# A graph attention and a DiT block on one core: graph maxima moved to PSUM, both outputs in one pair of banks, and four steps placed elsewhere in the written order

## The chip, the cores and the metric

The kernel runs on one core of one Trainium2 chip. The metric is the device time of one execution in microseconds (us); lower is better. Before the change three runs took 708.34, 708.88 and 709.95 us, median 708.88.

## What is computed

The inputs are x with 64 graphs of 64 nodes and 256 features, a condition of 256 features for each graph, an integer adjacency of 64 x 64 x 11 for each graph, and weights. All arithmetic is fp32. Two blocks follow each other; the reference, cut to what matters:

```python
# 1. graph attention, M = 20 neighbours, H = 16 heads, two directions d
q_exp = where(v.sum(-1) == 0, 0, q)            # condition of each node
self_feat = concat([v, q_exp]) @ W_self.T + b_self
kv = self_feat[:, :20]
for d in range(2):                             # adjacency, or transposed
    aff = qh @ kh / 4                          # heads of 16 features
    aff = where(A.sum(-1) > 0, aff, NEG) + A @ w_bias + b_bias
    output += (softmax(aff) @ kv) @ Wout[d] + bout[d]
x = v + relu(self_feat + output)
# 2. DiT block; shift, scale, gate come from silu(cond) @ Wt + bt
h = layernorm(x) * (1 + scale_msa) + shift_msa
x = x + gate_msa * (attention(h) @ Wproj + bproj)     # 16 heads, 64 tokens
h = layernorm(x) * (1 + scale_mlp) + shift_mlp
x = x + gate_mlp * (gelu(h @ W1 + b1) @ W2 + b2)
```

## The kernel before

**Groups, tiles and slots.** The 64 graphs are taken in nine groups (`NB`, line 26): 4, seven times 8, and 4 graphs. A group of 8 has 512 tokens in four tiles of 128. The order of all work is written out by hand: the scheduler is switched off (line 72), so each engine executes its instructions in the order in which the Python functions issue them, and waits in place for what an instruction needs. `start` (line 987) brings in groups 0 and 1, then for g = 1 to 7 a `boundary(g)` (line 826) and a `period(g)` (line 927) follow, then `finish` (line 1106).

In `period(g)` three stages of three groups run together: the DiT attention of group g, the graph attention of group g + 1 and the MLP of group g - 1; group g + 2 is prepared as well. The period has a slot for each of the four tiles, and `slot` (line 781) fixes what one does:

- TensorE writes the scores of a DiT tile (L657) and of a graph tile (L493) to two pairs of PSUM banks, `sca` (tag "pa") and `scb` (tag "pb"). DiT scores take columns 0 to 255 of each bank, graph scores 256 to 415.
- `block_exp`: VectorE takes maxima (L668) and subtracts them (L670), ScalarE the exponential (L674). `block_normal`: sum (L678), reciprocal (L679), GpSimd's product (L680).
- `graph_masked`: VectorE multiplies scores by the mask into `w` (L504), GpSimd adds the term (L509). `graph_exp`: maxima into `mx` in SBUF (L514), subtraction in `w` (L515), exponential (L516). `graph_normal`: L521, L522, L523.
- The tiles of the slot before are finished: transposes (ppT, L687, and pwT, L531), `block_attended` into a new pair "pao" with tag "pa" (L698, evacuated by ScalarE at L708), and `graph_output` into a new pair "po" with tag "pb" (L549; evacuated by L556, or L558 and L559; GpSimd adds at L560).

Between these lie places named p, f0, f1, d0, f2, f2b, d1, d2 and f3, and `fills` (line 948) says which further steps stand in each place of each slot: `mlp_up` (pu, L749, with its gelu L751), `mlp_down` (py, L759), `block_proj` (pproj, L731, then L721 and L740), `mlp_gated` and `mlp_out` (L721, L773 and the output DMA L775), LayerNorms, mask steps (L382 to L395), and the making of group g + 2's features: `self_cond` (on GpSimd, two products tq, L350, that need row flags fetched by a DMA, nzb), `self_product` (pf, L359) and `self_features` (L366 on VectorE, which empties pf's bank, and a copy to kv on GpSimd, L367).

A LayerNorm is three steps: `norm_stats` (L578, L579, then four small GpSimd operations to L585), `normed` (xn on ScalarE, L591) and `modulated` (phT on TensorE, L599; L602 on VectorE; L606 on GpSimd). `half_normed` and `second_normed` call them for the first and the second LayerNorm; hT and h2T hold the results, and `block_qk` (pqk, L619) reads hT.

**Banks.** Four PSUM banks beside the two pairs are handed out in turn by `bank` (line 90); py keeps one for as long as it accumulates. A step that gets a bank waits until the one that had it last has been read. In the second slot of a steady period the two pf get the same bank, as only two others are handed out between them.

**Buffers by tag.** A new tile of a tag waits until every reader of the one before it is done. So the scores of a slot wait for the evacuation of "pao" and "po" of the slot before.

**DMA.** Loads, gates and outputs are issued on SP, in the written order. `load_gate` brings the gates that `biased` (L714, on GpSimd) and `gated` (L721) read.

Of the kernel before, what the change touches and what calls it, by code (L numbers as in the profile page):

```python
# [9 lines left out]
F32 = mybir.dt.float32  # L10
# [7 lines left out]
P = 128  # L18
# [28 lines left out]
def graph_attention_then_dit_block(  # L47
# [49 lines left out]
    def pair(which, name):  # L97
        return ps.tile([P, 2, 512], F32, tag=which, name=name)
# [383 lines left out]
    def graph_scores(g, j, sc, first=4 * N):  # L482

        G = groups[g]
        t = Tile()
        t.g, t.j = g, j
        t.pa = [p_[:, :, ds(first, 8 * M)] for p_ in sc]
        kblk = G.kblk[j]
        for d in range(2):
            for c in range(2):  # L490
                for r in range(2):
                    for s in range(2):
                        nc.tensor.matmul(  # L493
                            t.pa[d][ts(s, N), r, ts(c, 4 * M)],
                            G.qT[ts(r, 64), d, c, ds(j * P + s * N, N)],
                            kblk[ts(r, 64), d, c, s, :], start=True, stop=True,
                        )
        return t
# [11 lines left out]

    def graph_exp(t):
        wf = t.w.rearrange("p h d m -> p (h d) m")
        mx = small.tile([P, 2 * H], F32, tag="mx", name="mx")
        nc.vector.tensor_reduce(mx, wf, AX.X, ALU.max)  # L514
        nc.vector.tensor_tensor(wf, wf, mx.unsqueeze(2).to_broadcast([P, 2 * H, M]), ALU.subtract)  # L515
        nc.scalar.activation(wf, wf, AF.Exp)  # L516
# [264 lines left out]
    def slot(e, c, e_next, c_next, before, fill):  # L781
        Eb, Cb = before
        fill("p")
        sc = [pair("pa", "sca"), pair("pb", "scb")] if e or c else None
        E = block_scores(*e, sc) if e else None
        C = graph_scores(*c, sc) if c else None
        if Eb:
            block_turned(Eb)
        elif Cb:
            graph_turned(Cb[0])  # L790
        fill("f0")
        if e_next:
            block_keys(*e_next)
        if c_next and c_next[0] != 1:
            graph_keys(*c_next)
        if E:
            block_exp(E)
        if c_next and c_next[0] == 1:
            graph_keys(*c_next)
        if C:  # L800
            graph_masked(C)
        fill("f1")
        if Eb and Cb:
            graph_turned(Cb[0])
        if E:
            block_normal(E)
        fill("d0")
        if C:
            graph_exp(C)
        if Eb:  # L810
            block_attended(Eb, pair("pa", "pao")[:, 0])
        fill("f2")
        po = pair("pb", "po") if Cb else None
        for i, t in enumerate(Cb):
            if i > 0:
                graph_turned(t)
            graph_output(t, po[:, i])
        fill("f2b")
        fill("d1")
        if C:  # L820
            graph_normal(C)
        fill("d2")
        fill("f3")
        return E, [C] if C else []

    def boundary(g, before):

        Eb, Cb = before
        n, a = g + 1, g + 2
        G, A = groups[g], groups[g - 1]  # L830
        last = A.nt // 2 - 1
        graph_k(n, 0)
        if g >= 2:
            mlp_gated(g - 2, len(groups[g - 2].parts) - 1)
        graph_v(n, 1)
        if g == 2:
            second_normed(g - 1, 0, 0)
        for i in range(0 if g == 2 else 4, 7):
            mask_step(n, i)
        if g >= 2:  # L840
            mlp_out(g - 2, len(groups[g - 2].parts) - 1)
        block_turned(Eb)
        for t in Cb:
            graph_turned(t)
        if g == 2:
            second_normed(g - 1, 0, 1)
        graph_q(n, 0, 0)
        block_attended(Eb, pair("pa", "pao")[:, 0])
        for t in Cb:
            graph_output(t, pair("pb", "po")[:, 0])  # L850
        graph_v_spread(n)
        graph_q(n, 0, 1)
        if last:
            second_normed(g - 1, 0, 2)
        if a < NG:
            load_adj(a)
            load_x(a)
        to_tokens(g, 1)
        if a < NG:
            load_xT(a)  # L860
        norm_stats(G, G.x1[1])
        block_proj(g - 1, last, later=True)
        normed(G, G.x1[1])
        block_added(g - 1, last)
        graph_q(n, 1, 0)
        graph_k(n, 1)
        modulated(G, G.hT, 1, amp1, off1, g)
        graph_q(n, 1, 1)
        second_normed(g - 1, last, 0)
        graph_keys(n, 0)  # L870
        block_qk(g, 1, 0)
        block_qk(g, 1, 1)
        block_keys(g, 0)
        second_normed(g - 1, last, 1)
        block_qk(g, 0, 0)
        second_normed(g - 1, last, 2)
        block_qk(g, 0, 1)
        block_v(g, 0)
        if a < NG:
            nonzero_rows(a)  # L880
        if g >= 2 and a < NG:
            mask_step(a, 0)
        load_gate(0, g, 0)
        for j2 in range(A.nt // 2):
            load_gate(1, g - 1, j2)
# [16 lines left out]
    def second_normed(g, j2, step):  # L902

        G = groups[g]
        if step == 0:
            second[g] = Tile()
            norm_stats(second[g], G.x1[j2])
        elif step == 1:
            normed(second[g], G.x1[j2])
        else:  # L910
            if j2 == 0:
                G.h2T = new_hT("hT" if g == NG - 1 else "h2T")
            modulated(second[g], G.h2T, j2, amp2, off2, g)
# [13 lines left out]
    def period(g):  # L927

        m, n, a = g - 1, g + 1, g + 2
        G = groups[g]  # L930

        def up(*ms):
            return [(mlp_up, m, i) for i in ms]

        def down(part, *ms):
            return [(mlp_down, m, part) + ms] if part < len(groups[m].parts) else []

        def masks(*steps):
            return [(mask_step, a, i) for i in steps] if g > 1 and a < NG else []

        def ahead(f, *args):
            return [(f, a) + args] if a < NG else []

        def bias_2(j2):
            return [(biased, 1, m, j2)] if j2 < len(groups[m].parts) else []

        gated_0 = [(mlp_gated, m, 0), (mlp_out, m, 0)] if g > 1 else []
        fills = [
            {
                "f1": [(block_v, g, 1)],  # L950
                "d2": masks(1) + ahead(self_cond, 0) + ahead(self_cond, 1),
                "f3": up(0, 1) + (up(2, 3) if g > 1 else []),
            },
            {
                "f0": ahead(self_product, 0) + (up(2, 3) if g == 1 else []) + down(0, 0, 1),
                "f1": ahead(self_features, 0),
                "f2b": ahead(self_product, 1),
                "d1": ahead(self_features, 1),
                "d2": masks(2, 3) + [(biased, 0, g, 0)],
                "f3": up(4, 5),  # L960
            },
            {
                "f0": down(0, 2, 3),
                "f1": down(0, 4, 5),
                "f2": ahead(graph_v, 0),
                "d2": bias_2(0) if g > 1 else [],
                "f3": [(block_proj, g, 0)] + up(6, 7),
            },
            {
                "f0": [(half_normed, n, 0)] + down(0, 6) + [(load_gate, 0, g, 1)],  # L970
                "f1": down(0, 7) + gated_0 + [(half_normed, n, 1)],
                "d0": [(half_normed, n, 2)],
                "f2": down(1, 0, 1, 2),
                "f2b": [(second_normed, g, 0, 0)] if g > 1 else [],
                "d2": bias_2(1 if g > 1 else 0),
                "f3": down(1, 3, 4) + [(half_normed, n, 3)] + ([(second_normed, g, 0, 1)] if g > 1 else []) + down(1, 5, 6, 7)
                + [(biased, 0, g, 1)],
            },
        ]
        if n == NG - 1:  # L980

            fills = fills[:3]
            fills[2]["f3"] = [(block_proj, g, 0)] + up(6) + [(half_normed, n, 0)] + up(7) + [(half_normed, n, 1), (load_gate, 0, g, 1)]
        slots = [((g, j), (n, j) if j < groups[n].nt else None) for j in range(G.nt)]
        return run_slots(slots, fills, (None, []))

    def start():
# [71 lines left out]
        for t in t1:  # L1059
# [36 lines left out]
                "f2": [(graph_v, 2, 0)],  # L1096
                "d0": [(half_normed, 1, 2)],
                "f2b": [(load_gate, 0, 0, 0)],
                "f3": [
                    (time_projection, 4), (biased, 0, 0, 0), (half_normed, 1, 3), (time_projection, 5),  # L1100
                ],
            },
        ]
        return run_slots([((0, 0), (1, 2)), ((0, 1), (1, 3))], fills, (None, t1))
# [154 lines left out]
```

## Time and profile before

| | |
|---|---|
| median of 3 runs | 708.88 us (708.34 to 709.95) |
| the profiled execution's own time | 711.31 us |
| its span, first to last instruction | 709.5 us |
| mean granted TensorE clock | 0.983 |
| TensorE busy with matmuls | 671.2 us, 95% |
| VectorE, ScalarE, GpSimd busy | 453.1, 377.0, 435.5 us |
| first scores of periods 1 to 7 at | 114.7, 194.9, 275.3, 355.1, 435.7, 515.8, 592.4 us |

Lines of the profile are read thus. A line of a stage has the stretch in us from the span's start, its length, then busy time and number of instructions for PE (matmuls), PEld (weight loads), DVE (VectorE), ACT (ScalarE) and POOL (GpSimd), then the granted TensorE clock (1.00 is full), the DMA engines' share and GB/s. A line of the order in time has start and duration in us, the engine, the source line, the operation, output <- input, their shapes and a count of instructions drawn together; brackets at the end give the idle time of the engine just before and what ended it. fp32 matmuls appear as two passes each. The end of a matmul is modelled: two that follow each other overlap in the listing, and their pace is the distance of their starts.

### The profile page before, as it was taken

Reading aid. Unit: us, or ns where it says so; the run is one execution under the profiler, and the core shown is the slowest. Engines: PE = TensorE matmul, PEld = TensorE weight load, DVE = VectorE, ACT = ScalarE, POOL = GpSimd, SP = SyncE. Lnnn points to the kernel's source line nnn. Section 1 sums busy time; section 2 is a strip of 40 time slices with the busy share of each in tenths; the row PEclk is TensorE's granted clock in tenths of the full one; section 3 lists DMA queues with packets and bytes.
Section 4 is the critical chain, followed back from the end, with each engine's and each line's share of the span. In section 5 each row is a group of like instructions: output and inputs, shape, how many; then the busy total and the mean of one; then the engine's idle time right before and its main releaser. Section 6 shows DMA issues by size and latency. Waiting matters only on the chain.

```text
span 709.5 us, 16045 instructions
## 1 busy us (share of the span) xinstructions
PE 671.2 (95%) x6624; PEld 456.8 (64%) x6624; DVE 453.1 (64%) x755; ACT 377.0 (53%) x675; POOL 435.5 (61%) x501
## 2 busy tenths in 40 slices
PE   8998899897999999999999999999999989899997
PEld 7655565585566765577556775568566765567576
DVE  4968845679388755878488755878378755654210
ACT  3353444665465654765465654666466645854412
POOL 7446345667657675668658675678557684547430
PEclk9997999999999999999999999999999999999999
DMA  9345140310441140410431240510321240011210
GB/s 283 103 123 175 53 141 2 76 46 13 136 83 25 60 147 3 105 46 21 144 69 37 61 128 21 106 46 20 90 69 30 56 113 2 3 46 29 77 43 30
DMA packets 45712, 50.74 MB, mean 72 GB/s; under 512 B 6761, under 2 KB 32937, under 8 KB 45641
## 3 DMA queue, kind: packets, MB, share of 16 engines
q1 hardware_dynamic: 44040, 48.26, 24.8%
q8 instruction: 52, 0.85, 0.6%
q0 software_dynamic: 368, 0.60, 0.4%
q10 hardware_dynamic: 1232, 0.87, 0.4%
q14 instruction: 20, 0.16, 0.1%
HBM read 42.63 MB, written 7.09 MB: 70 GB/s over the span
## 4 chain that ended last, share of the span: by engine, by line
PE 57%; DVE 15%; ACT 9%; POOL 8%; DMA 7%; issue 3%; SPq 0%; ACTq 0%; POOLq 0%; DVEq 0%
PE py L759 12%; PE pqk L619 7%; PE pu L749 7%; PE pqT L457 5%; DVE w L515 4%; PE pproj L731 4%; PE ppT L687 3%; PE pwT L531 3%; DMA nzd<-nz 3%; DMA nzb<-nzd 2%; PE pf L359 2%; PE phT L599 2%; PE po L549 2%; PE pk L442 2%; DVE mx L514 2%
## 5 line engine op out<-in xcount | busy, mean ns | idle before, releaser
L759 PE MATMUL py<-w,u 128*128 128x256 f32 x512 | 123.0, 386 | 0.2 <-ACT u L751 0.2
L749 PE MATMUL pu<-h2T,w 128*128 128x512 f32 (+1 forms) x256 | 108.2, 567 | 0.2 <-POOL h2T L606 0.2
L759 PEld LDWEIGHTS py<-w,u 128*128 128x128 f32 x512 | 95.4, 192 | 17.3 <-issue 3.8
L509 POOL TENSOR_TENSOR w<-w,term 128x640 f32<-128x640 f32 x32 | 49.4, 1546 | 63.4 <-DVE w L504 23.8
L749 PEld LDWEIGHTS pu<-h2T,w 128*128 128x128 f32 x256 | 48.4, 191 | 46.5 <-issue 44.4
L680 POOL TENSOR_TENSOR pr<-pr,sm 128x1024 f32<-128x1024 f32 x32 | 60.8, 1900 | 10.5 <-DVE sm L679 8.8
L751 ACT ACTIVATE u<-pu,vec 128x512 f32<-128x512 f32 (+1 forms) x72 | 43.2, 639 | 44.4 <-PE pu L749 44.3
L516 ACT ACTIVATE w<-w 128x640 f32<-128x640 f32 x32 | 23.4, 734 | 76.8 <-DVE w L515 76.8
L591 ACT ACTIVATE xn<-x,shift,rstd 128x256 f32<-128x256 f32 x64 | 34.8, 592 | 51.5 <-POOL shift L585 51.5
L619 PE MATMUL pqk<-hT,wqkv 128*128 128x512 f32 (+1 forms) x144 | 58.7, 551 | 3.2 <-POOL hT L606 3.2
L457 PE MATMUL pqT<-sfT,wq 128*128 128x512 f32 (+1 forms) x144 | 60.8, 550 | 0.0
L560 POOL TENSOR_TENSOR xT<-xT,sfT 128x256 f32<-128x256 f32 x32 | 23.7, 742 | 59.7 <-ACT sfT L559 37.4
L523 POOL TENSOR_TENSOR w<-w,sm 128x640 f32<-128x640 f32 x32 | 43.4, 1358 | 27.0 <-DVE sm L522 27.0
L515 DVE TENSOR_TENSOR w<-w,mx 128x640 f32<-128x640 f32 x32 | 52.9, 1653 | 1.1
L678 DVE TENSOR_REDUCE sm<-pr 128x16 f32<-128x1024 f32 x32 | 38.8, 1212 | 22.1 <-ACT pr L674 20.2
L602 DVE TENSOR_TENSOR h2T<-phT,amp 128x512 f32<-128x512 f32 x15 | 10.4, 690 | 58.1 <-PE phT L599 58.1
L687 PE MATMUL ppT<-ident,pr 128*128 128x128 f32 x256 | 37.2, 285 | 10.3 <-ACT u L751 4.5
L674 ACT ACTIVATE pr<-pr 128x1024 f32<-128x1024 f32 x32 | 33.8, 1058 | 22.6 <-DVE pr L670 22.4
L714 POOL TENSOR_TENSOR x<-x,gates 128x512 f32<-128x512 f32 x32 | 42.4, 1325 | 5.1 <-DMA gates<-gate 5.1
L619 PEld LDWEIGHTS pqk<-hT,wqkv 128*128 128x128 f32 x144 | 26.0, 190 | 29.9 <-issue 20.1
L668 DVE TENSOR_REDUCE mx<-sca 128x8 f32<-128x512 f32 x32 | 21.9, 683 | 36.1 <-PE sca L493 35.6
L690 ACT COPY pT<-ppT 128x512 f32<-128x512 f32 x64 | 34.5, 595 | 18.3 <-PE ppT L687 18.3
(149 smaller groups left out, 1476.7 us busy)
## 6 DMA issues: line engine op xcount, KB each, us to landing
gates<-gate SPq DMA_DIRECT2D x64, 256.0 KB
out<-x SPq DMA_DIRECT2D x15, 256.0 KB
xT<-in_x_t SPq DMA_DIRECT2D x7, 512.0 KB
a_d<-in_adj SPq DMA_DIRECT2D x7, 440.0 KB
a_d<-in_adj_t SPq DMA_DIRECT2D x7, 440.0 KB
x_g<-in_x SPq DMA_DIRECT2D x11, 256.0 KB
vblk<-vd SPq DMA_DIRECT2D x28, 80.0 KB
w<-in_w SPq DMA_DIRECT2D x2, 1024.0 KB
```

The lines of the kernel that those rows point to most:

```text
L457: nc.tensor.matmul(pq, wq_sb[d][:, k, ts(c, P)], G.sfT[:, k, :], start=(k == 0), stop=(k == 1))
L509: nc.gpsimd.tensor_tensor(t.w, t.w, G.term[:, :, j, :].unsqueeze(1).to_broadcast([P, H, 2, M]), ALU.add)
L515: nc.vector.tensor_tensor(wf, wf, mx.unsqueeze(2).to_broadcast([P, 2 * H, M]), ALU.subtract)
L523: nc.gpsimd.tensor_tensor(wf, wf, sm.unsqueeze(2).to_broadcast([P, 2 * H, M]), ALU.mult)
L619: nc.tensor.matmul(pp, wqkv_sb[:, k, ds(i * D + c * P, P)], G.hT[:, k, 0 : G.T], start=(k == 0), stop=(k == 1))
L678: nc.vector.tensor_reduce(sm, t.pr, AX.X, ALU.add)
L680: nc.gpsimd.tensor_tensor(t.pr, t.pr, sm.unsqueeze(2).to_broadcast([P, H, N]), ALU.mult)
L687: nc.tensor.transpose(pt[:, ts(i, P)], t.pr[:, ts(q4 * 4 + i, 2), :].rearrange("p h m -> p (h m)"), ident)
L714: nc.gpsimd.tensor_tensor(G.x1[j2], G.x1[j2], G.gates[which, j2][:, :, 1, :], ALU.add)
L749: nc.tensor.matmul(pu, w1_sb[:, k, ts(m, P)], G.h2T[:, k, 0 : G.T], start=(k == 0), stop=(k == 1))
L751: nc.scalar.activation(G.u[m], pu, AF.Gelu, bias=col("b1", m))
L759: nc.tensor.matmul(G.py[:, ts(i, D)], G.u[m][:, ts(t, P)], w2_sb[:, m, :], start=(m == 0 and i == 0), stop=(m == 7), skip_group_check=True,)
```

## The change

Six edits, of which the last four only place steps elsewhere:

1. `graph_exp` keeps its maxima `mx` in PSUM for groups from 1 on: 32 columns of the second bank of scb, behind the scores (columns 448 to 479, or 416 to 447 for a tile whose scores start at column 0).
2. In a slot one pair with tag "pa" takes the block's attended output (first bank) and the graph's output (second bank); the slot no longer takes a pair with tag "pb" for the latter.
3. In a period, `self_cond` moves from the end of the first slot to place f1 of the second, `self_product(0)` from f0 to f1, `self_features(0)` from f1 to d0, `self_product(1)` from f2b to f2. In period 1, `mlp_up` 2 and 3 move from the second slot to the end of the first.
4. In the tail of `start`, `half_normed(1, 3)` moves ahead of `time_projection(4)`, and `biased(0, 0, 0)` moves to boundary 1.
5. In period 1 `block_proj(1, 0)` leaves the third slot, and boundary 2 takes it; the second LayerNorm of group 1's first half, spread over the front of boundary 2 before, now stands among the `block_qk`.
6. In period 6 `mlp_down` 6 and 7 of the last part leave the fourth slot; boundary 7 takes them, and with them `mlp_gated` and `mlp_out`.

```diff
@@ graph_scores
+        t.mx = sc[1][:, 1, ds(first // 8 + 4 * N + 8 * M, 2 * H)] if g > 0 else None
@@ graph_exp
-        mx = small.tile([P, 2 * H], F32, tag="mx", name="mx")
+        mx = small.tile([P, 2 * H], F32, tag="mx", name="mx") if t.mx is None else t.mx
@@ slot
+        po = pair("pa", "po") if Eb or Cb else None
         if Eb:
-            block_attended(Eb, pair("pa", "pao")[:, 0])
+            block_attended(Eb, po[:, 0])
         fill("f2")
-        po = pair("pb", "po") if Cb else None
         for i, t in enumerate(Cb):
             if i > 0:
                 graph_turned(t)
-            graph_output(t, po[:, i])
+            graph_output(t, po[:, 1 if Eb else i])
@@ boundary
         graph_k(n, 0)
-        if g >= 2:
+        rest = [6, 7] if g == NG - 2 else []
+        if g >= 2 and not rest:
             mlp_gated(g - 2, len(groups[g - 2].parts) - 1)
         graph_v(n, 1)
-        if g == 2:
-            second_normed(g - 1, 0, 0)
         for i in range(0 if g == 2 else 4, 7):
             mask_step(n, i)
-        if g >= 2:
+        if g >= 2 and not rest:
             mlp_out(g - 2, len(groups[g - 2].parts) - 1)
         block_turned(Eb)
         for t in Cb:
             graph_turned(t)
-        if g == 2:
-            second_normed(g - 1, 0, 1)
         graph_q(n, 0, 0)
...
         graph_q(n, 0, 1)
-        if last:
+        if g == 2:
+            block_proj(1, 0)
+        elif last:
             second_normed(g - 1, 0, 2)
...
+        if rest:
+            mlp_down(g - 2, 1, rest[0])
         to_tokens(g, 1)
...
         normed(G, G.x1[1])
+        if g == 1:
+            biased(0, 0, 0)
         block_added(g - 1, last)
         graph_q(n, 1, 0)
         graph_k(n, 1)
+        if rest:
+            mlp_down(g - 2, 1, rest[1])
         modulated(G, G.hT, 1, amp1, off1, g)
+        if rest:
+            mlp_gated(g - 2, 1)
+            mlp_out(g - 2, 1)
         graph_q(n, 1, 1)
-        second_normed(g - 1, last, 0)
+        if g == 2:
+            second_normed(1, 0, 0)
+            second_normed(1, 0, 1)
+        else:
+            second_normed(g - 1, last, 0)
         graph_keys(n, 0)
         block_qk(g, 1, 0)
+        if g == 2:
+            second_normed(1, 0, 2)
+            second_normed(1, 1, 0)
         block_qk(g, 1, 1)
@@ period, fills of the slots
-                "d2": masks(1) + ahead(self_cond, 0) + ahead(self_cond, 1),
-                "f3": up(0, 1) + (up(2, 3) if g > 1 else []),
+                "d2": masks(1),
+                "f3": up(0, 1, 2, 3),
             },
             {
-                "f0": ahead(self_product, 0) + (up(2, 3) if g == 1 else []) + down(0, 0, 1),
-                "f1": ahead(self_features, 0),
-                "f2b": ahead(self_product, 1),
+                "f0": down(0, 0, 1),
+                "f1": ahead(self_cond, 0) + ahead(self_cond, 1) + ahead(self_product, 0),
+                "d0": ahead(self_features, 0),
+                "f2": ahead(self_product, 1),
...
-                "f3": [(block_proj, g, 0)] + up(6, 7),
+                "f3": ([(block_proj, g, 0)] if g > 1 else []) + up(6, 7),
...
-                "f3": down(1, 3, 4) + [(half_normed, n, 3)] + ([(second_normed, g, 0, 1)] if g > 1 else []) + down(1, 5, 6, 7)
+                "f3": down(1, 3, 4) + [(half_normed, n, 3)] + ([(second_normed, g, 0, 1)] if g > 1 else []) + down(1, *((5, 6, 7) if n < NG - 2 else (5,)))
@@ start, fills of its last slot
-                "f3": [
-                    (time_projection, 4), (biased, 0, 0, 0), (half_normed, 1, 3), (time_projection, 5),
-                ],
+                "f3": [(half_normed, 1, 3), (time_projection, 4), (time_projection, 5)],
```

## The prediction

> **What bounds the kernel now.** I read the page's busy shares first, then the busy time of each engine by stage, then the order in time inside one stage.
>
> ```profile
> PE 671.2 (95%) x6624; PEld 456.8 (64%) x6624; DVE 453.1 (64%) x755; ACT 377.0 (53%) x675; POOL 435.5 (61%) x501
> ```
>
> TensorE is the bound: 709.5 - 671.2 = 38.3 us without a matmul. The stages show where (first pair the stretch, then its length, then PE).
>
> ```profile
> 78.00:114.73 36.73, 33.98 (x265) 21.50 (x265) 20.43 (x39) 16.57 (x33) 19.98 (x28) 0.95 0.29 90
> 114.73:140.31 25.58, 21.21 (x262) 15.29 (x261) 17.90 (x25) 13.39 (x25) 13.60 (x12) 0.93 0.27 53
> 140.31:167.49 27.18, 24.25 (x372) 19.55 (x373) 20.59 (x34) 18.53 (x32) 18.08 (x20) 1.00 0.10 31
> 167.49:194.90 27.41, 25.21 (x156) 14.71 (x156) 16.38 (x31) 12.29 (x24) 19.86 (x28) 1.00 0.32 96
> 194.90:274.90 80.00, 78.93 (x804) 52.23 (x804) 55.99 (x93) 46.23 (x80) 54.14 (x61) 1.00 0.27 70
> ...
> 592.35:624.00 31.65, 28.69 (x325) 18.90 (x328) 21.52 (x31) 20.57 (x34) 15.66 (x14) 0.95 0.01 2
> ```
>
> A steady period (194.90 on) has 1.1 us of idle PE in 80; the others, to 515.7, have 0.7 to 1.3. What a faster VectorE can give there is that and no more. The idle PE time lies in groups 1 and 2 (78 to 195) and in the last full group (592 to 624), where the granted clock (third number from the end) also falls below 1. The second slot of a steady group, before:
>
> ```profile
> 365.24 0.34 PE L657 MATMUL sca<-kb,qk 32*64 32x128 f32 x4
> ...
> 367.12 1.14 PE L687 MATMUL ppT<-ident,pr 128*128 128x128 f32 x8 [0.48 <-ACT u L751]
> ...
> 368.19 1.98 PE L359 MATMUL pf<-xT,w_self 128*128 128x512 f32 x4
> ...
> 369.56 2.04 POOL L350 TENSOR_TENSOR tq<-nzb,qwT 128x512 f32<-128x512 f32 x2 [1.28 <-DMA nzb<-nzd]
> ...
> 370.63 0.75 DVE L366 SCALAR_TENSOR_TENSOR sfT<-pf,vec,tq 128x512 f32<-128x512 f32 x1 [0.31 <-POOL tq L350]
> ...
> 372.70 0.65 PE L698 MATMUL pao<-pT,v 128*32 128x64 f32 x32
> ...
> 373.91 1.98 PE L359 MATMUL pf<-xT,w_self 128*128 128x512 f32 x4
> ```
>
> The second pf comes 3 us after the addition L366 that empties the first one's bank. The subtraction of the graph maxima (L515), with GpSimd at work and without:
>
> ```profile
> 361.57 1.90 POOL L680 TENSOR_TENSOR pr<-pr,sm 128x1024 f32<-128x1024 f32 x1 [0.30 <-issue]
> 362.16 1.99 DVE L515 TENSOR_TENSOR w<-w,mx 128x640 f32<-128x640 f32 x1
> ```
>
> ```profile
> 562.92 0.82 DVE L515 TENSOR_TENSOR w<-w,mx 128x640 f32<-128x640 f32 x1
> 562.98 0.82 POOL L585 TENSOR_TENSOR shift<-shift,rstd 128x2 f32<-128x2 f32 x1
> ```
>
> It lasts 0.82 us alone, 1.92 at the median of 32, and where it starts inside L680 it ends 0.7 us after L680 does.
>
> **What the Trainium skill says.** "SBUF — State Buffer", Who interferes with whom: a VectorE instruction with two SBUF inputs contends with a GpSimd instruction that reads SBUF, and the later one waits for the whole of the other; with one SBUF input it does not. The two fences agree. "PSUM — Partial Sum Buffer", Specifications: VectorE may write 4-byte types to PSUM and take one tensor input from there; mx would be the only one. "TensorE: Matmul & The Clock Gate", What's actually happening: after an idle window of about 3.4 us the array runs at half rate. The trace agrees in kind: after waits of 1.71 and 2.20 us, with 1.1 us of transposes between, four passes from 126.43 took 3.4 us instead of the 1.73 that the same four take elsewhere; so one such stretch costs about 1.7 us. A wait of 2.00 at 88.7 brought one too, one of 2.07 at 167.5 did not.
>
> **The edits, on this execution's own clock.**
>
> *Maxima in PSUM.* 30 of 32 subtractions lose their second SBUF input. Estimate 0.82 us: L504, PSUM and SBUF in, takes 0.48 for 320 columns and L670 0.68 for 512, so 640 come to 0.81. Bounds: 0.8, or 1.9 if nothing changes. The reduction (0.79) keeps its length, give or take 0.05. In exchange the bank of scb is held until the subtraction has read it; the next scores come at least 2 us later, except for group 1's first two tiles, where it ends at 51.1 and the next scb scores stand at 50.95: at most 0.1, and PE waits there for ScalarE until 51.65 anyway.
>
> *Both outputs in the pair of sca.* sca is free of its readers (L670, L504) as early as scb; the next sca scores now wait for the later of two evacuations (aoT and L558/L556). The aoT copy was the later one at 379.7 already (scores waited 0.36). Zero, covered by the 3.5 us of pu ahead of the scores.
>
> *Cond's part in the second slot, groups 1 to 6.* The two tq (2.04 us) leave the front of POOL's queue, where they waited 1.28 us for a DMA with kb, kblk and L509 behind them. They now stand behind L509, the copies to kv behind L680. On DVE the first addition L366 moves behind the sum and reciprocal of the block's softmax, and on PE the second pf moves ahead of po, still in the bank of the first. From the slot's start S: PE reaches it after scores 1.40, ppT 1.07, py 1.73, pf 1.82, pwT 0.96, pao 0.47 = S+7.45. DVE's part: first maximum at S+1.20 (355.11 to 356.31), two maxima and two subtractions 2.47, table load with its lead 1.46, exponential 1.06, sum and reciprocal 1.55, addition 0.75 and 0.13 of hand-overs = S+8.62. A new wait of 1.17 us; po, pu and the next scores are behind it. Bounds: 0.3 (a slower PE start) and 2. In group 6 pf has half the columns: PE is 0.9 earlier, the addition 0.27 shorter: 1.8.
> Idle PE in the slots of groups 2 to 6 before, less 0.2 at each boundary: 0.9 + 0.5 + 1.1 + 0.7 + 0.65 = 3.9; it hung on the late L515 (L516, then gelu or aoT, then PE) and goes. New: 4 x 1.17 + 1.8 = 6.5. Net **+2.6**.
>
> *Group 1's second slot.* up(2,3) moves ahead (1.73 us, neither lost nor won). Waits before: 1.71 + 2.20 + 0.46, and 1.7 of half clock: 6.1. After: gelu starts 1.2 earlier (L515 122.6, exponential 123.4, table 124.7, u0 125.15), PE would be at ppT at 122.87: 2.3; then 0.1; pf 1.0. That is 3.4, and scores, wait and transposes make 4.8 us with little matmul, so I take the half clock again (1.7): **-1.0**; without it -2.7.
>
> *Tail of the start (78 to 92).* L515 ends at 82.3, not 83.9. With hT ahead of the time projections, L602 ends at 85.1 instead of 88.6. PE loses 0.4 in front of phT (xn ends at 82.5) and 0.7 in front of the second half of ppT (the gate's addition, 87.7); pqT starts at about 89.4, not 92.14: **-2.7** (-1.0 if the 0.7 tips the clock). biased(0,0,0) no longer holds POOL for its gates (2.3 us); its new place puts 1.3 us ahead of L740, and L606 ends 0.05 later.
>
> *Group 2's boundary.* pproj (1.73) moves there from the third slot. The third slot's 0.33 goes. In the fourth, L602 follows L515 by way of exponential, sum and reciprocal: 1.2 of the 2.07 goes. In the boundary the first LayerNorm's xn no longer stands ahead of aoT on ACT (it waited 4.6 us for POOL there): phT's 0.6 and pxT's 1.4 go, with six VectorE mask steps 1.2 us earlier. Behind it both LayerNorms now follow each other within four pqk: phT waits 0.6 for the first xn and 1.0 for the second, bounds 0.5 and 3.5 together. -3.5 + 1.6 = **-1.9**.
>
> *Last boundary.* py 6 and 7 (0.86 each) fill 0.4, 0.7 and part of 1.04, but slot four shrinks only 0.6, as pwT then waits for L523 on POOL (569.8): **-0.5**. The group's last L721 and L773 go behind hT (0.69 on DVE, 1.26 on POOL); the LayerNorm behind them has 3 us to spare until ScalarE reaches its xn. Its output DMA, now behind the vblk loads on SP, is waited for by no one.
>
> *Group 7's slots.* ppT's 0.47 and the scores' 0.58 go, the following ppT's 0.97 stays: about -1.3 with what else moves; the clock stretch at 617.7 (1.7) goes in half of the cases: **-2.2**.
>
> Sum: 2.6 - 1.0 - 2.7 - 1.9 - 0.5 - 2.2 = -5.7, on a span of 709.5 in an execution of 711.31. The runs' median is 708.88 with 708.34 to 709.95, and I take the difference over: 703.2.
>
> **Rivals.** (1) *Slower:* the new wait in front of the second pf tips the clock. pwT, pao and the wait make 2.6 us without dense matmuls. Six groups at 1.7 are +10.2: 713.4; it decides from five of six on (+8.5, 711.7). Against: scores, wait and ppT, 2.95 us, never tip it in slots 1 today. Chance 0.13. (2) *The subtraction is not shortened:* the 3.9 stays, so +6.5; start -1.1, group 1 +0.2, group 2 -0.7, last -0.5, group 7 0: +4.4, 713.3. Against: L504 and L670 beside POOL. Chance 0.04. (3) *Early gains given back:* clock tips at the start (+1.7) and once later (+1.7), group 2's LayerNorms cost 3.5 instead of 1.6 (+1.9): -0.4, 708.5. Chance 0.15. (4) *The pf wait is 0.3 and group 1 keeps its clock:* -5.0 - 1.7 more: 696.5. Chance 0.08.
>
> **How the numbers follow.** The forecast, 0.60, lies between 699.5 and 707. About 0.2% (1.4 us) is what a measurement of this kernel can tell from no change. Faster: 0.60 + 0.08 + a third of (3), 0.05 = 0.73; same: the rest of (3), 0.10; slower: 0.17. The range 696.5 to 709.0 leaves out (1) and (2).
>
> **What would show it.** L515 at about 0.82 with POOL busy; no ppT wait for u in slots 1; PE waiting about 1.2 us for L366's successor ahead of the second pf, in each of groups 2 to 5; pqT near 89.4; scores of group 2 some 5.6 us earlier than 194.9. Wrong if that pf wait exceeds 2 us, if granted clock below 1 appears in the steady groups, or if the two LayerNorms hold pqk for more than 2 us.

## The result, and the profile after

The change makes the kernel slower: four runs took 740.06 to 744.44 us, median 743.26, beside 707.7 to 709.95, median 708.61, for the kernel before. The ratio is 1.048, with a 95% interval of 1.044 to 1.052. Forecast were 703.2 us and a range of 696.5 to 709.0. The profiled execution took 744.44 us with a span of 742.6 us and a mean granted clock of 0.964 (0.983 before). In what follows line numbers are those of the kernel after: up to L487 as before, then, in all lines named here, two higher (L515 is L517, L708 is L710).

First the busy shares:

```profile
PE 681.1 (92%) x6624; PEld 463.5 (62%) x6624; DVE 422.9 (57%) x755; ACT 380.1 (51%) x675; POOL 428.1 (58%) x501
```

VectorE lost the 30 us that the edit was meant to take from it. TensorE, with the same number of instructions, is busy 9.9 us longer and idle 61.5 us instead of 38.3. So look at what it waits for (us in total, times, longest):

```profile
PE po L551 <- ACT aoT L710: 25.8, 17, 4.5
PE po L547 <- ACT aoT L710: 9.1, 4, 4.4
...
PE pf L359 <- DVE sfT L366: 4.0, 6, 1.1
```

The pf wait is the one that the prediction foresaw. The two lines above it, 34.9 us in 21 waits, are new, and no step of the prediction has them: the graph's output (L547 and L551 write `po`) waits for ScalarE's copy `aoT` (L710) of the *attended* output, which is the other half of the same pair. A fourth slot of a steady group, in order of time:

```profile
416.35 0.65 PE L700 MATMUL po<-pT,v 128*32 128x64 f32 x32
...
416.93 2.86 PE L761 MATMUL py<-w,u 128*128 128x256 f32 x12
...
419.76 1.09 ACT L593 ACTIVATE xn<-x,shift,rstd 128x256 f32<-128x256 f32 x2 [1.84 <-POOL shift L587]
...
420.75 0.72 ACT L518 ACTIVATE w<-w 128x640 f32<-128x640 f32 x1
...
421.38 0.60 ACT L710 ACTIVATE aoT<-po,vec 128x128 f32<-128x128 f32 x2
422.04 0.75 PE L551 MATMUL po<-wT,vblk 80*32 80x64 f32 x32 [2.25 <-ACT aoT L710]
422.71 3.01 PE L761 MATMUL py<-w,u 128*128 128x256 f32 x8
...
429.25 1.25 PE L442 MATMUL pk<-kv,wk 128*128 128x160 f32 x8
```

The same slot before:

```profile
404.48 0.75 PE L549 MATMUL po<-wT,vblk 80*32 80x64 f32 x32
...
405.13 1.09 ACT L591 ACTIVATE xn<-x,shift,rstd 128x256 f32<-128x256 f32 x2 [2.45 <-POOL shift L585]
405.16 1.99 PE L759 MATMUL py<-w,u 128*128 128x256 f32 x8
...
406.75 0.60 ACT L708 ACTIVATE aoT<-pao,vec 128x128 f32<-128x128 f32 x2
...
410.02 1.25 PE L442 MATMUL pk<-kv,wk 128*128 128x160 f32 x8
```

Read them side by side. The attended output is finished at 417.0, and its copy could follow within 1 us (it does in experiment 3). It comes at 421.38, since ScalarE executes in the written order and has `xn` (waiting for GpSimd) and the exponential of `w` (waiting for VectorE's subtraction) in front of it. Before, the copy was as late, 406.75, but the graph output did not care: it ran 2.3 us *earlier*, at 404.48. Now it stands behind it. And behind the wait the same eight passes py take 3.01 us instead of 1.99; from py to pk 6.54 us go by instead of 4.86. That is half clock, 1.68 us: the granted clock is 0.50 from 423.54 to 426.96.

By stage, from first scores to first scores: start and group 0 +2.8, first two slots of group 1 -2.3, its rest and boundary +3.6, groups 2 to 6 +26.5, the rest +2.5; together 33.1, the difference of the spans. The first of these is the least certain: at the first scores of group 1 the change stands at 117.55 us, and experiments 10 and 12, whose code is the same up to there, at 115.85 and 115.70.

### The profile page after: what moved, and what is told of

Same layout as the page of the kernel before. It is cut to its first block, busy times and chain, and to the rows that moved or that the text cites. A ratio compares the mean times of both kernels' runs of the same rounds, so it can differ in the third digit from the quotient of the medians.

```text
span 742.6 us, 16046 instructions
## 1 busy us (share of the span) xinstructions
PE 681.1 (92%) x6624; PEld 463.5 (62%) x6624; DVE 422.9 (57%) x755; ACT 380.1 (51%) x675; POOL 428.1 (58%) x501
## 4 chain that ended last, share of the span: by engine, by line
PE 59%; DVE 17%; ACT 11%; POOL 8%; issue 2%; DMA 2%; ACTq 0%; POOLq 0%; DVEq 0%
PE pu L751 12%; PE py L761 9%; PE pqk L621 7%; PE pqT L457 5%; PE pproj L733 3%; PE po L551 3%; PE pv L629 3%; DVE mx L670 3%; DVE w L517 3%; PE phT L601 3%; PE pk L442 2%; DVE sm L680 2%; PE ppT L689 2%; DVE pr L672 2%; ACT w L518 2%
## 5 line engine op out<-in xcount | busy, mean ns | idle before, releaser
L761 PE MATMUL py<-w,u 128*128 128x256 f32 x512 | 126.8, 394 | 0.2 <-ACT u L753 0.2
L751 PE MATMUL pu<-h2T,w 128*128 128x512 f32 (+1 forms) x256 | 113.8, 590 | 0.6 <-ACT v L636 0.4
L761 PEld LDWEIGHTS py<-w,u 128*128 128x128 f32 x512 | 97.0, 197 | 15.5 <-issue 1.8
L682 POOL TENSOR_TENSOR pr<-pr,sm 128x1024 f32<-128x1024 f32 x32 | 60.8, 1900 | 17.2 <-DVE sm L681 15.6
L593 ACT ACTIVATE xn<-x,shift,rstd 128x256 f32<-128x256 f32 x64 | 34.9, 592 | 45.5 <-POOL shift L587 45.5
L551 PE MATMUL po<-wT,vblk 80*32 80x64 f32 x1024 | 24.8, 241 | 25.8 <-ACT aoT L710 25.8
L621 PEld LDWEIGHTS pqk<-hT,wqkv 128*128 128x128 f32 x144 | 25.9, 190 | 29.3 <-issue 19.6
L551 PEld LDWEIGHTS po<-wT,vblk 80*32 80x32 f32 x1024 | 20.3, 152 | 37.5 <-ACT aoT L710 36.1
```

Of the source, the lines that this page charges most:

```text
L551: nc.tensor.matmul(po[ts(i, 32), ds(c * P + s * N, N)], vblk[:, 2 * j + s, :, :, 4 * c + i].rearrange("p h e -> p (h e)"), t.wT[:, 4 * c + ...
L621: nc.tensor.matmul(pp, wqkv_sb[:, k, ds(i * D + c * P, P)], G.hT[:, k, 0 : G.T], start=(k == 0), stop=(k == 1))
L682: nc.gpsimd.tensor_tensor(t.pr, t.pr, sm.unsqueeze(2).to_broadcast([P, H, N]), ALU.mult)
L751: nc.tensor.matmul(pu, w1_sb[:, k, ts(m, P)], G.h2T[:, k, 0 : G.T], start=(k == 0), stop=(k == 1))
L761: nc.tensor.matmul(G.py[:, ts(i, D)], G.u[m][:, ts(t, P)], w2_sb[:, m, :], start=(m == 0 and i == 0), stop=(m == 7), skip_group_check=True,)
```

## The experiments

Theory A: the shared pair makes the graph output wait for aoT, late on ScalarE, and the half clock follows these waits. Rival B: the pf wait of the moved cond part, or the clock that it tips. Rival C: the maxima in PSUM, or the moved LayerNorms. Each ratio is to the kernel before on the same chip, in brackets its 95% interval.

**1. The shared pair taken back.**

```diff
-        po = pair("pa", "po") if Eb or Cb else None
         if Eb:
-            block_attended(Eb, po[:, 0])
+            block_attended(Eb, pair("pa", "pao")[:, 0])
         fill("f2")
+        po = pair("pb", "po") if Cb else None
...
-            graph_output(t, po[:, 1 if Eb else i])
+            graph_output(t, po[:, i])
```

> The changed kernel with one edit undone: pao goes to the pair of sca and po to the pair of scb again; all else stays. Theory A (shared tile: the graph output waits for the attended output's evacuation L710 although the two lie in different banks, and L710 stands on ScalarE behind exp of w): the 21 waits of po on aoT, 34.9 us, go and with them the half-clock stretches; the output now waits for the subtraction that reads mx in the same pair, which ends 0.5 us before po's turn in second and third slots and 0.6 after it in fourth ones. 703 to 709. Rival B (the wait of the second pf, or the half clock that it brings, is the cause): 735 to 744. Rival C (mx in PSUM, or the moved LayerNorms): above 730.

Measured: 702.11 us, 0.988 (0.984 to 0.992). The aoT waits are gone, with B and C all still in place. In their stead po waits 11.7 us in all, for the subtraction that reads mx from its pair (in part the profile names another releaser; in the fourth slot at 237 us, po starts 0.15 us after that subtraction ends).

**2. The shared pair alone, on the kernel before** (the same lines, the other way round).

> The kernel before with one edit alone: both outputs in one pair of banks. Theory A: the output of a fourth slot, at 404.5 in the trace of before, would wait for an evacuation that ends at 407.4 there, 2.9 us in each of five or more groups and 1 to 2 us in other slots, where the subtraction is the long one of 1.9 us; with half clock behind the long waits 740 to 760. Rivals B and C: within 2 us of the kernel before, 709.

Measured: 801.35 us, 1.128 (1.124 to 1.131). The edit alone costs 90 us (801.35 against 710.89 on the same chip); A holds in kind, and its size was far off. The po waits come to 79.7 us, longest 6.8. My estimate was taken from a fourth slot. In second slots the chain in front of aoT is longer: tq on GpSimd, then L509, then a subtraction of 1.9 us, then the exponential; one po waits 5.66 us there. In the whole change, which has the short subtraction and the moved tq, the steady second slots wait 0.94 us; which of the two does more was not tried apart.

**3. The shared pair kept, ScalarE's order changed.**

```diff
+        po = pair("pa", "po") if Eb or Cb else None
+        if Eb:
+            block_attended(Eb, po[:, 0])
         fill("d0")
         if C:
             graph_exp(C)
-        po = pair("pa", "po") if Eb or Cb else None
-        if Eb:
-            block_attended(Eb, po[:, 0])
         fill("f2")
```

> The changed kernel, still with both outputs in one pair, but the attended output is written down ahead of the graph's maxima and exponential and of the fillers before them, so that only ScalarE's order changes: L710 stands ahead of exp(w) and of the LayerNorm's xn. Theory A: the evacuation ends some 1.1 us after pwT's copies and before po's turn, the po waits fall from 34.9 us to under 3, steady periods come back to about 80 us: 702 to 706. If sharing a pair costs in some other way than through ScalarE's order (two writers of one pair, or its banks held longer for the next scores): above 730. Rival B: 735 to 744.

Measured: 696.38 us, 0.980 (0.976 to 0.984), 47 us under the change. TensorE, VectorE and GpSimd have the same instructions in the same order; ScalarE alone takes aoT earlier. Its fourth slot:

```profile
391.82 0.62 ACT L710 ACTIVATE aoT<-po,vec 128x128 f32<-128x128 f32 x2
...
393.72 0.74 PE L551 MATMUL po<-wT,vblk 80*32 80x64 f32 x32
393.75 1.09 ACT L593 ACTIVATE xn<-x,shift,rstd 128x256 f32<-128x256 f32 x2 [1.31 <-POOL shift L587]
...
394.75 0.72 ACT L518 ACTIVATE w<-w 128x640 f32<-128x640 f32 x1
```

The copy ends 1.3 us before the output starts, and there is no wait. All po waits on aoT fall from 34.9 to 3.8 us. The spans of the two profiled executions differ by 48.7 us: idle PE falls from 61.5 to 30.8 (30.7), busy PE from 681.1 to 663.1 (18.0). The second part is mostly half clock: at a mean granted clock of 0.964 the change loses 742.6 x 0.036 = 26.7 us, experiment 3 at 0.989 only 693.9 x 0.011 = 7.6, both counted through idle time too.

**4. A tile of its own for the graph output.**

```diff
-            graph_output(t, po[:, 1 if Eb else i])
+            graph_output(t, bank("po") if Eb else po[:, i])
```

(and the attended output in a pair "pao" with tag "pa").

> The changed kernel with the graph output in one of the four rotating banks, so that neither the pair of mx nor the attended output is in its way. Theory A: 702 to 706, without the po waits on aoT and without a wait on the subtraction. If the rotation is the scarcer thing (pu or pf then meets a bank not yet evacuated): 708 to 725, with waits of pu or py for the rectifier of the graph output. Rival B: 735 to 744.

Measured: 694.87 us, 0.978 (0.975 to 0.982). aoT is as late on ScalarE as in the change (10.43 us into a fourth slot in both), and the output no longer waits for it. So the late order on ScalarE costs nothing by itself, and experiment 3 shows that writing both halves of one pair costs nothing by itself either. It takes the two together: a late reader of one half, and a writer of the other half of the same tile of the program. "PSUM — Partial Sum Buffer", Summary: rules for kernel authors, asks for a different bank, guarded bank by bank, where PSUM is read while a matmul writes. The two halves are different banks; the guard here covered the pair. No run puts the two outputs into two tiles on neighbouring banks, so that it is the tile and not the neighbourhood is argued, from this and from experiment 11, where po in a first bank waits for a reader of a second one.

**5. What the maxima in PSUM are worth.** Experiment 3 with `t.mx = None`, so mx lies in SBUF.

> The changed kernel with the attended output ahead of the maxima (as in e3_attended_first, 696.4) and the maxima in SBUF again: what the maxima in PSUM are worth once nothing waits behind the subtraction. The prediction priced the long subtraction at 10.1 us between its forecast and its rival 2, most of it by way of ScalarE's aoT, which stands ahead of the exponential here. If it was right: 703 to 707, with subtractions of 1.9 us back. If the aoT place was the whole path: 696 to 699, and the maxima in PSUM are worth nothing by themselves.

Measured: 709.44 us, 0.999 (0.997 to 1.001). So they are worth 13.1 us (709.44 - 696.38) beside the other edits, nearly the whole gain over the kernel before, though aoT stands ahead of the exponential. The upper half of my expectation was 2 us too low; the second reading falls.

**6. Cond's part back in its old places,** in experiment 3 (edit 3 of the change undone).

> e3_attended_first with cond's part back where the kernel before has it (tq at the end of the first slot, both products of the second slot apart, up(2,3) of group 1 in the second slot). The second pf then waits for no addition: the 3.5 us of pf waits on L366 go. If that is all: 692.5 to 694. If the move brought as much elsewhere (GpSimd's front free for kb and kblk, group 1's second slot without its wait for gelu): 696 to 701.

Measured: 695.76 us, 0.980 (0.978 to 0.982): no difference from experiment 3. The pf waits are gone, and po waits for aoT 8.2 us instead of 3.8. Neither reading is right alone: the move costs its pf wait, and without it other waits grow by about as much.

**7. The moved work alone** (edits 4 to 6 on the kernel before).

> The kernel before with the moved work alone: LayerNorms, block_proj and bias of group 2's boundary, and the last group's rest of the MLP; maxima in SBUF, outputs in two pairs, cond's part in its old place. The prediction's terms for these edits come to -1.9 - 0.5 and part of -2.7 and -2.2: 703 to 707. If they cost (two LayerNorms within four products of keys): 709 to 713.

Measured: 709.33 us, 0.999 (0.998 to 1.000), no difference that counts. Rival C's second half falls, and so does a gain from these edits by themselves.

**8. The second pf behind the graph output,** in experiment 3 (`self_product(1)` from f2 to f2b).

> e3_attended_first with the second slot's second product pf behind the graph output instead of ahead of it, its addition still behind. The addition L366 ends at 7.9 us of the slot and the output would start at 7.3 and run 0.7, so pf meets an emptied bank: the pf waits of 3.5 us go, and nothing else moves: 692 to 694. If the output's copies of wT were late then (they end 7.4 us into the slot), 0.1 to 0.3 us a group stays: 694 to 695. If pf was not on the path: 696.

Measured: 697.43 us, 0.982 (0.978 to 0.985): no gain to be seen. The pf waits go, and the po waits on aoT rise from 3.8 to 8.2 us. A wait was put off, not taken away.

**9. Three edits together**: 3, 4 and 8.

> Three things together: graph output in a rotating bank (as in e4_own_bank, 694.9), attended output ahead of the maxima (as in e3_attended_first, 696.4), second pf behind the graph output (as in e8_first_pf_last). The output can't wait for aoT any more (6.0 us in e8_first_pf_last) and pf not for its addition: 690 to 694. If those waits are only put off to a later one (scores, gelu): 694 to 697.

Measured: 691.29 us, 0.973 (0.970 to 0.976), the fastest of all and 2.7% under the kernel before. TensorE is idle for 29.3 us of 690.2. In second slots po now waits 0.66 us for the copies of wT, so a part was put off once more.

**10. The wait filled.** In fourth slots of the changed kernel, ahead of the output:

```diff
+        if Eb and Eb.j == 2:
+            over = bank("over")
+            for _ in range(5):
+                nc.tensor.matmul(over, ident, w1_sb[:, 0, 0:512], start=True, stop=True)
```

> The changed kernel with five products of 128x512 added, whose result nobody reads, in front of the graph output of every fourth slot (groups 1 to 6), where TensorE waits 2.25 us for aoT, 4.4 in group 1. They take 2.16 us. Theory A's second half (half clock follows the wait, since TensorE has nothing to do): the output comes no later, and the half-clock stretch behind it goes in five groups or six, 1.7 us each: 733 to 736 in spite of the added work. If the half clock has another cause: 743 to 746, and if the added work is not hidden: 750 to 757.

Measured: 741.83 us, 1.045 (1.041 to 1.049). A miss by my arithmetic: five fp32 products are ten passes, 4.46 us, twice the 2.16 that I counted. The output came 13.06 us into the slot, not 11.09, so 1.97 us were lost, and the half clock, 1.68, was gone all the same (4.86 us from py to pk). The two nearly cancel: a steady group takes 85.6 us, and 85.3 in the change.

**11. The maxima in PSUM alone,** on the kernel before (edit 1).

> The kernel before with one edit alone: the maxima in PSUM beside the scores, outputs in two pairs. The graph output then waits for the subtraction that reads mx in its pair, as in e1_two_pairs, 11.7 us of such waits there. The shorter subtraction was worth 13 us with the attended output first. If it is worth that here too, less the waits: 702 to 706. If the waits eat it: 708 to 712.

Measured: 739.88 us, 1.041 (1.037 to 1.045). Both readings were wrong by 30 us. A second slot (here L516 is the subtraction, L510 GpSimd's term, L550 the output):

```profile
381.98 2.05 POOL L350 TENSOR_TENSOR tq<-nzb,qwT 128x512 f32<-128x512 f32 x2 [3.21 <-DMA nzb<-nzd]
...
386.33 1.53 POOL L510 TENSOR_TENSOR w<-w,term 128x640 f32<-128x640 f32 x1
...
388.76 0.82 DVE L516 TENSOR_TENSOR w<-w,scb 128x640 f32<-128x640 f32 x1
...
389.68 1.09 PE L550 MATMUL po<-wT,vblk 80*32 80x64 f32 x32 [5.46 <-issue]
390.70 3.78 PE L359 MATMUL pf<-xT,w_self 128*128 128x512 f32 x4
```

po gets the pair in which mx lies, and waits for L516, 5.46 us (the profile says "issue"; the wait ends 0.1 us after L516 does). L516 waits for L510, and L510 stands behind tq, which waited for its DMA. Then half clock: pf takes 3.78 us instead of 1.98. All waits of po together come to 39 us. So the edits of this change lean on each other: the maxima in PSUM need po out of their pair (edit 2) or, by experiment 1, which has edits 3 to 6 as well, tq out of the way; that it is edit 3 there and not another was not tried alone.

**12. The wait filled, in the right measure**: two products of 512 columns and one of 256.

> As e10_wait_filled, with the added products cut to what the wait holds: two of 128x512 and one of 128x256, 2.16 us by the 4.46 us that five took there. Theory A's second half: the output comes when it did in the changed kernel, the half-clock stretch of 1.68 us behind it is gone in groups 2 to 5, perhaps in group 1: 735 to 737. If the added products move the output as they did there: 741 to 744. If the half clock comes back, since 2.16 us of products don't count: 743.

Measured: 734.38 us, 1.033 (1.031 to 1.035).

```profile
413.05 2.31 PE L819 MATMUL over<-w,ident 128*128 128x512 f32 x6
...
414.81 0.60 ACT L710 ACTIVATE aoT<-po,vec 128x128 f32<-128x128 f32 x2
...
415.46 0.74 PE L551 MATMUL po<-wT,vblk 80*32 80x64 f32 x32
416.13 1.99 PE L761 MATMUL py<-w,u 128*128 128x256 f32 x8
...
420.99 1.25 PE L442 MATMUL pk<-kv,wk 128*128 128x160 f32 x8
```

aoT and po come when they did, 11.09 us into the slot, and py is back at 1.99 us, py to pk at 4.86. Work that nobody needs, 2.16 us in six places, makes the kernel 8.9 us *faster* (743.26 - 734.38); a steady group takes 83.6 us instead of 85.3, which is 1.7 us in each of groups 2 to 5. The half clock there is a consequence of TensorE's idle time in the wait.

## Why the prediction was wrong

**The step that failed** is "Both outputs in the pair of sca ... Zero, covered by the 3.5 us of pu ahead of the scores". It asked when the *next scores* may write the pair, which had indeed room. It did not ask who else writes it: the second half is written, by TensorE, in the same slot, after ScalarE was given the first half to read. The step even had the late copy in hand ("The aoT copy was the later one at 379.7 already"), and ScalarE's order (exponential, then aoT) was in the profile. Experiment 3 against the change prices the missing term at +47 us, about two thirds of it idle TensorE and a third busy time, mostly at half clock. One of the prediction's signs of being wrong did show, a granted clock below 1 in the steady groups, but this wait brought it and not the one that the prediction had in mind.

**Without that term** the rest was too careful. Experiment 3 is the change less nearly all of this wait; its stages against the forecast:

| stage | forecast | measured |
|---|---|---|
| start, to the first scores of group 1 | -2.7 | -3.5 |
| group 1, first two slots | -1.0 | -2.4 |
| group 1, rest and boundary | -1.9 | -2.5 |
| groups 2 to 6 | +2.6 | -4.1 |
| last boundary and after | -2.7 | -3.1 |
| sum | -5.7 | -15.6 |

- *Maxima in PSUM*: the price was right.

```profile
L517 DVE TENSOR_TENSOR w<-w,scb 128x640 f32<-128x640 f32 x30 | 24.6, 821 | 1.0
```

  0.82 us by estimate and by measurement, and the reduction at 0.79 as said. The worth was 13.1 us rather than the 10.1 between the forecast and rival 2.
- *Groups 2 to 6*: the new pf wait is 0.61 us, not 1.17 (1.08 in group 6, not 1.8). TensorE came as worked out (S + 7.33 against 7.45); VectorE's chain ended at S + 7.89, not 8.62, since ScalarE loads its table beside the second subtraction: from the end of the subtractions to the exponential 0.90 us pass, not 1.46. The idle time that goes was put at 3.9 and comes to 4.1 + 3.5 = 7.6: I had counted gaps in the matmul rows alone, and taken what a faster VectorE can give for "that and no more". Part of the old waiting lies inside a modelled duration: over these groups PE counts as busy for 390.6 us before and 387.6 in experiment 3, with the same matmuls and the clock at 1.00 in both. In the third slot of the kernel before:

```profile
390.04 2.30 PE L731 MATMUL pproj<-wproj,aoT 128*128 128x256 f32 x8
...
391.21 0.73 PEld L731 LDWEIGHTS pproj<-wproj,aoT 128*128 128x128 f32 x4 [0.44 <-ACT aoT L708]
```

  The matmul row shows no gap, but takes 2.30 us where it takes 1.99 after the change, and the weight load inside it waits 0.44 us for the late aoT.
- *Group 1's second slot*: in experiment 3 a wait of 1.33 us for gelu and none at the second pf, instead of the 2.3 and 1.0 forecast; the half clock stayed, as taken (clock 0.75 from 123 to 128). In the change itself it was 1.33 and 0.50 us, at full clock (1.00 from 124 to 134.5).
- *Start*: pqT stands at 88.64 in experiment 3 (89.4 forecast), known to some 2 us as said above. In the change an aoT wait of 3.07 us eats it.
- *Group 2's boundary*: -1.9 was nearly right, but comes only with the short subtraction: with the old one the moved work gains nothing there (experiment 7: 55.3 us for this stage, and 54.6 in the kernel before).
- *Rival 1* put a slower outcome on the clock behind the pf wait. That wait exists and never tips it in experiment 3: the clock is 1.00 through groups 2 to 6. In the change it had a share once: in group 6's second slot its 1.08 us and the aoT wait of 1.80 us behind it were followed by half clock. What made the change slower was in none of the rivals.

One question remains: why does a wait of 2.25 us bring half clock in the fourth slots of groups 2 to 5, and one of 2.24 us at the same place in group 6 not? "TensorE: Matmul & The Clock Gate", What's actually happening, says that the window over which activity is watched runs freely and is some 3.4 us long. The clock in these traces agrees. In the change, half clock begins in the four groups at 252.88, 338.21, 423.54 and 508.88 us, 85.33 us apart, and ends 3.41 us later; 85.33 is 25 times 3.413, and every other stretch of half clock in this trace begins on the same grid. Here are three steps of the grid around the wait from 419.79 to 422.04, then the step in group 6 (the column after POOL is the clock):

```profile
420.13:423.54 3.41, 1.50 (x36) 1.36 (x37) 0.78 (x3) 2.02 (x6) 1.45 (x1) 1.00 0.00 0
423.54:426.96 3.42, 3.42 (x12) 2.78 (x11) 2.21 (x7) 1.22 (x3) 2.93 (x6) 0.50 0.00 0
426.96:430.37 3.41, 3.41 (x20) 3.02 (x18) 1.04 (x2) 0.12 (x1) 3.41 (x4) 1.00 0.00 0
594.21:597.63 3.42, 2.53 (x41) 2.21 (x42) 1.58 (x6) 1.25 (x4) 1.13 (x3) 1.00 0.05 15
```

In each of groups 2 to 5 one step holds 1.9 to 2.0 us of the wait and the narrow matmuls of po behind it; TensorE is busy for 1.44 to 1.54 us of it, and half clock follows. In group 6 a point of the grid, 594.21, cuts the wait into 1.35 and 0.89 us. The fourth slots of experiment 2 fit. The point cuts each of its waits of 2.85 or 2.86 us too: 2.03 and 1.75 us of it fall behind the point in groups 4 and 6, and half clock follows; in groups 2, 3 and 5 it is 0.87, 1.28 and 1.58 us, and none does. So where a wait falls counts beside its length, and a step need not be wholly idle. How busy a step has to be stays open, and busy time alone does not decide: ahead of the point in group 2 of experiment 2, a step with only 1.42 us of matmuls, all of them wide (from 269.78), brought no half clock, and in experiment 3 one with 2.01 us (from 118.66), most of them narrow, did.

## What to carry to other kernels

When two results are put into one tile to free a buffer, ask for each half not only when the next owner may write, but who writes the other half while the first is read, and what stands ahead of that reader on its engine. A late copy that nobody waits for costs nothing until an edit makes somebody wait for it: so before merging buffers, move such copies up in their engine's order, or give each result a tile of its own. And price a wait of TensorE near 2 us twice, with and without 1.7 us of half clock behind it: here the same wait had both outcomes.

## What was not expected of the hardware

Adding 2.16 us of unneeded matmuls to a wait of 2.25 us took 1.68 us off the work behind it (experiment 12): the same eight passes took 1.99 instead of 3.01 us. Of five waits of 2.85 or 2.86 us at one and the same place (experiment 2, fourth slots), two had half clock behind them and three did not, by where the grid of 3.41 us cut them. And one edit of a few lines, the shared pair, cost 90 us alone and 47 with the others, without adding a matmul.
